# A four-layer graph network on one core: where a relu, the totals rows, some casts and the small weight loads stand, and how cell weights are loaded

## Chip, cores and metric

The kernel runs on one core of a Trainium2 chip. The metric is device time in microseconds of one execution; lower is better. The engines are named as the profile names them: PE multiplies matrices (PEld is its weight load), DVE is the vector engine, ACT the scalar engine, POOL is GpSimd, SP issues DMAs.

## What is computed

3327 nodes with 64 features go through four residual layers. Each layer normalizes its input, applies a relu, propagates over the same adjacency matrix and adds the result to `x`.

```python
def _ggc(x, adj, W, wih, whh, bih, bhh):
    m = adj @ (x @ W)
    gi = m @ wih.T + bih
    gh = x @ whh.T + bhh
    i_r, i_z, i_n = jnp.split(gi, 3, axis=-1)
    h_r, h_z, h_n = jnp.split(gh, 3, axis=-1)
    r = jax.nn.sigmoid(i_r + h_r)
    z = jax.nn.sigmoid(i_z + h_z)
    n = jnp.tanh(i_n + r * h_n)
    return (1.0 - z) * n + z * x
# layer 0: relu(_ggc(relu(_ggc(h, adj, cell 1)), adj, cell 2))
# layer 1: weights 0.5 ** (how many neighbours stand behind this one in the row,
#          the last 100 only), times (h @ weight), plus bias
# layer 2: three times  x = (adj * adj) @ x;  x = x @ W.T + b
# layer 3: twice  x = tanh(concat(adj @ x, x) @ W[k])
# each layer: h = max(layernorm(x), 0);  x = x + layer(h, adj)
```

So the adjacency is used eight times: two plain passes (the two GRU cells), one ranked pass (layer 1), three squared passes and two plain ones.

## The kernel before

The nodes are padded to 3328, 26 blocks of 128 rows. A tile is one block of source rows against half of the destination columns: group 0 holds chunks 0 and 1 (3 blocks each), group 1 holds chunks 2 and 3 (3 and 4 blocks). With its two halves of destinations a tile of group 0 is 768 KB, one of group 1 is 896 KB. There are 20 slots for tiles in SBUF, and most tiles are loaded several times. A joint loop runs two passes over the same tiles, so that a load serves both: `alone(0, 0)`, then `joint(1, 0)` (passes 0 and 1 on group 1), `joint(0, 1)` (passes 1 and 2 on group 0), `joint(1, 2)`, and so on to `alone(0, 7)`. Pass 2 is the ranked one.

The order of the instructions on each engine is that of the program's text as it is emitted: every engine runs its own list in that order. The text is interleaved by hand. The main loop `run` emits units (pass, chunk, tile) of matmuls. Everything else, such as what follows the last tile of a chunk, is a generator that `yield`s an amount of microseconds; each unit "spends" its own share of matmul time on the open generators (`STREAM_US * w / CWM`, 0.645 for a plain unit of three blocks, 0.806 for a ranked one), and a generator whose amount is used up emits its next piece. A larger number after `yield` thus means that the next piece stands later in the lists of its engines, whatever the clock says.

The pieces that the change touches:

- `more_constants` (line 190) sets up constants in the background. `load_cell` (148) loads the weights of a GRU cell with four DMAs: W and the three input gates twice into `folds` (lines 152), once for each half of the partitions, and the three hidden gates twice into `cells` (153). The bias columns `bcol` are loaded twice (199). `fold_cell` (155) multiplies W with the input gates on PE, with a factor 0.5, since both halves of the partitions hold the same weights. `bd` and `w3` (232, 234) are the weights of layers 1 to 3, six small DMAs.
- `make_mask` (405) turns a tile into a bf16 mask of nonzeros for the ranked pass, in two pieces on DVE (411, one for each half); the pieces wait in a queue and are emitted one or more for each unit. Row 127 of the mask is not a mask but the row counts `totals`, which POOL copies in by DMA (416), emitted with the first piece.
- `expand` (429) makes ranks out of masks: PE multiplies the mask with a triangle `tri` (a `mm`, line 255), and a relu takes the result from PSUM to an int16 tile `e`, on ACT (461) or DVE (459). It runs three units ahead of the matmuls that use `e` (546).
- `gru` (781) is the cell: the accumulators are copied out (741, 742), PE forms the gates (792), ACT the sigmoids and the tanh (797, 813), DVE the rest (802 to 819). After cell 0 the relu of the new state is written in two halves, one on ACT (822), one on DVE (823); then `after_0` brings it back to nodes with matmuls (707).
- `after_1` (870) follows cell 1: `gru`, transposes, residual, `layernorm_relu` (its power is on POOL, 761), and `in_three` (829), which splits the result in three bf16 terms for the ranked pass: two casts on ACT (841), two subtractions on DVE (843).

## Time and profile before

| | |
|---|---|
| time, median of 3 runs | 721.32 us (717.43 to 722.89) |
| span of the profiled run | 714.8 us |
| granted TensorE clock | 1.00 |
| HBM read | 199.68 MB, 281 GB/s over the span |

The page gives for each engine its busy time, then slices of the span, queues, the chain that ended last, and the costliest groups. Matmuls in float32 are two records each, and the ends of matmuls are modelled, so a busy PE may still be waiting a little; gaps in the timeline tell more. The matmuls with the adjacency (line 546) are the largest group by far. The rest of the large groups is the work that feeds the ranked and the squared passes:

```profile
L546 PE MATMUL sum<-adj,y 128*64 128x384 f32 (+3 forms) x3016 | 532.6, 503 | 13.2 <-DMA adj<-in_adjT 12.2
L546 PE MATMUL sum<-e,adj 128*64 128x384 bf16 (+1 forms) x624 | 72.6, 339 | 0.6 <-DVE e L459 0.6
L388 ACT ACTIVATE adj<-adj 128x768 f32<-128x768 f32 (+1 forms) x173 | 141.9, 891 | 50.3 <-PE sum L546 26.9
L411 DVE TENSOR_SCALAR adj<-adj 128x768 bf16<-128x768 f32 (+3 forms) x208 | 114.8, 603 | 33.5 <-PE temp L481 29.6
```

A row reads: line, engine, operation, what it writes and reads, the commonest shape, how many; busy us and mean ns of one; idle time of its engine just before, and who ended it.

### The profile page before, as it was taken

Reading aid. Unit: us, or ns where it says so; the run is one execution under the profiler, and the core shown is the slowest. Engines: PE = TensorE matmul, PEld = TensorE weight load, DVE = VectorE, ACT = ScalarE, POOL = GpSimd, SP = SyncE. Lnnn points to the kernel's source line nnn. Section 1 sums busy time; section 2 is a strip of 40 time slices with the busy share of each in tenths; the row PEclk is TensorE's granted clock in tenths of the full one; section 3 lists DMA queues with packets and bytes.
Section 4 is the critical chain, followed back from the end, with each engine's and each line's share of the span. In section 5 each row is a group of like instructions: output and inputs, shape, how many; then the busy total and the mean of one; then the engine's idle time right before and its main releaser. Section 6 shows DMA issues by size and latency. Waiting matters only on the chain.

```text
span 714.8 us, 12622 instructions
## 1 busy us (share of the span) xinstructions
PE 685.6 (96%) x5112; PEld 344.0 (48%) x5112; DVE 344.0 (48%) x696; ACT 264.1 (37%) x402; POOL 76.7 (11%) x113
## 2 busy tenths in 40 slices
PE   4999899999999898999999999999999999999997
PEld 1545444555546586545444444334444444334464
DVE  6756636634987988658524102321163566005101
ACT  0114000212037666888998223740065600000101
POOL 3500000001390602121100000000010000000000
PEclk9999999999999999999999999999999999999999
DMA  9999996299586367662999749962998399927991
GB/s 347 401 363 404 405 406 196 64 351 397 186 298 236 115 205 262 211 239 72 313 368 366 255 146 408 405 263 79 375 373 259 113 397 405 404 82 263 403 402 39
DMA packets 69109, 201.54 MB, mean 282 GB/s; under 512 B 7404, under 2 KB 8788, under 8 KB 69052
## 3 DMA queue, kind: packets, MB, share of 16 engines
q1 hardware_dynamic: 66156, 199.70, 75.4%
q8 instruction: 40, 0.66, 0.4%
q10 hardware_dynamic: 720, 0.85, 0.3%
q0 software_dynamic: 2176, 0.20, 0.2%
q14 instruction: 17, 0.14, 0.1%
HBM read 199.68 MB, written 0.85 MB: 281 GB/s over the span
## 4 chain that ended last, share of the span: by engine, by line
PE 55%; DVE 2%; DMA 2%; ACT 0%; issue 0%; POOL 0%; ACTq 0%; DVEq 0%; SPq 0%; POOLq 0%
PE sum L546 51%; PE temp L255 3%; DMA adj<-totals 1%; PE temp L707 1%; DMA adj<-in_adjT 1%; DVE adj L411 1%; DVE both L742 0%; ACT both L741 0%; DVE e L459 0%; POOL st L761 0%; PE sum L255 0%; DVE xs L940 0%; DVE y L765 0%; DVE y L758 0%; DVE t L753 0%
## 5 line engine op out<-in xcount | busy, mean ns | idle before, releaser
L546 PE MATMUL sum<-adj,y 128*64 128x384 f32 (+3 forms) x3016 | 532.6, 503 | 13.2 <-DMA adj<-in_adjT 12.2
L546 PEld LDWEIGHTS sum<-adj,y 128*64 128x64 f32 x3016 | 221.5, 137 | 267.8 <-issue 223.9
L388 ACT ACTIVATE adj<-adj 128x768 f32<-128x768 f32 (+1 forms) x173 | 141.9, 891 | 50.3 <-PE sum L546 26.9
L411 DVE TENSOR_SCALAR adj<-adj 128x768 bf16<-128x768 f32 (+3 forms) x208 | 114.8, 603 | 33.5 <-PE temp L481 29.6
L461 ACT ACTIVATE e<-temp,bitsb 128x384 int16<-128x384 f32 (+1 forms) x114 | 65.3, 606 | 23.5 <-PE temp L255 14.6
L546 PE MATMUL sum<-e,adj 128*64 128x384 bf16 (+1 forms) x624 | 72.6, 339 | 0.6 <-DVE e L459 0.6
L742 DVE COPY both<-sum 64x384 f32<-64x384 f32 (+3 forms) x17 | 9.7, 569 | 118.7 <-ACT both L741 117.5
L741 ACT COPY both<-sum 64x384 f32<-64x384 f32 (+3 forms) x17 | 8.1, 477 | 155.2 <-PE sum L546 155.1
L390 DVE TENSOR_TENSOR adj<-adj 128x768 f32<-128x768 f32 (+1 forms) x35 | 33.6, 1006 | 51.1 <-DMA adj<-in_adjT 30.9
L255 PE MATMUL temp<-adj,tri 128*64 128x384 bf16 (+1 forms) x334 | 51.9, 342 | 5.5 <-DVE e L459 2.3
L761 POOL TENSOR_TENSOR st<-st,mhalf 128x6 f32<-128x6 f32 (+1 forms) x16 | 24.0, 1500 | 295.5 <-DVE st L760 295.5
L546 PEld LDWEIGHTS <-adj 128*64 128x64 bf16 x624 | 40.4, 110 | 18.5 <-issue 6.4
L416 POOL DMA_DIRECT2D adj<-totals x52 | 31.9, 615 | 133.5 <-DVE adj L819 75.0
L459 DVE TENSOR_SCALAR e<-temp 128x384 int16<-128x384 f32 (+1 forms) x53 | 31.8, 606 | 21.2 <-ACT e L461 8.6
L255 PEld LDWEIGHTS <-tri 128*64 128x64 bf16 x416 | 28.6, 109 | 25.8 <-issue 12.8
L736 DVE STREAM_TRANSPOSE both<-y 32x96 f32<-32x96 f32 (+1 forms) x128 | 35.6, 278 | 2.9
L688 DVE COPY t<-sum 128x384 f32<-128x384 f32 x8 | 4.4, 555 | 61.3 <-PE sum L546 61.3
L481 PE MATMUL temp<-adj,behind 128*64 128x384 bf16 x208 | 28.8, 339 | 0.6 <-DVE adj L411 0.4
L686 ACT COPY t<-sum 128x384 f32<-128x384 f32 (+1 forms) x8 | 4.2, 528 | 53.7 <-PE sum L546 53.7
L481 PEld LDWEIGHTS <-behind 128*64 128x64 bf16 x208 | 13.6, 110 | 21.1 <-issue 19.5
L903 DVE TENSOR_TENSOR y<-temp,brow 128x384 f32<-128x384 f32 (+1 forms) x8 | 4.7, 591 | 29.6 <-PE temp L255 29.6
L515 ACT ACTIVATE lastw<-adj,bitsb 128x768 int16<-128x768 f32 (+1 forms) x2 | 2.0, 984 | 44.1 <-DVE adj L513 44.1
(113 smaller groups left out, 330.1 us busy)
## 6 DMA issues: line engine op xcount, KB each, us to landing
adj<-in_adjT SPq DMA_DIRECT2D x130, 768.0 KB, 7.8
adj<-in_adjT SPq DMA_DIRECT2D x104, 896.0 KB, 12.4
xs<-in_x SPq DMA_DIRECT2D x1, 640.0 KB
adj<-totals POOLq DMA_DIRECT2D x26, 3.0 KB, 4.9
adj<-totals POOLq DMA_DIRECT2D x26, 3.5 KB, 3.0
out<-xs ACTq DMA_DIRECT2D x2, 192.0 KB, 4.0
folds<-in_weights SPq DMA_DIRECT2D x4, 64.0 KB, 12.1
out<-xs ACTq DMA_DIRECT2D x1, 256.0 KB
```

What stands on the lines that cost most here:

```text
L255: nc.tensor.matmul(out[hs], lhsT[:, hs], rhs, start=start, stop=stop)
L388: nc.scalar.activation(sq, v, AF.Square)
L390: nc.vector.tensor_tensor(sq, v, v, ALU.mult)
L411: nc.vector.tensor_scalar(t.mask.view[:rows, half], t.view()[:rows, half], 0.0, None, op0=ALU.not_equal)
L416: nc.gpsimd.dma_start(out=t.mask.view[P - 1:P], in_=totals[t.g][t.q:t.q + D + 1:D, :])
L459: nc.vector.tensor_scalar(wide[:, s], ps[:, :w], BITS, 0.0, op0=ALU.add, op1=ALU.max)
L461: nc.scalar.activation(wide[:, s], ps[:, :w], AF.Relu, bias=bitsb)
L481: nc.tensor.matmul(counts[c][1][s * D:(s + 1) * D, :w], behind[:, NQ - 1 - t.q:NQ - 1 - t.q + D], t.mask.view[:, s, t.cols(c)], start=firs ...
L546: nc.tensor.matmul(acc[h][1][h * D:(h + 1) * D, :w], yq[h], rhs[h], start=first and n == 0, stop=last and n == len(terms) - 1)
L736: nc.vector.transpose(to[at:at + 32, :, q], h[q * 32:(q + 1) * 32, :, s, f * 32:(f + 1) * 32])
L742: nc.vector.tensor_copy(both[c][upper(1), 1], acc[1][1][upper(1), :width(c)])
L761: nc.gpsimd.tensor_tensor(st[:, 3, :n], st[:, 2, :n], mhalf[:, :n], ALU.pow)
```

## The change

It rearranges what is small. The cell weights and the bias come once, into a tile `stage` that is zero in its lower half, and PE and DVE copy them to both halves of the partitions (`unfold_cell`); `fold_cell` works from `stage`. `bd` and `w3` are loaded after the second cell has been folded, and later. The DVE half of the cell's relu stands before the yield, and that yield is a little longer. The row of totals is asked for when the mask is planned, not with its first piece. Some relus of `expand` go from ACT to DVE: in group 1, the second half of tiles whose source is chunk 2. The casts of `in_three` stand later, and `after_1` has one pace of 1.25 for both groups.

```diff
-    folds = const.tile([P, 2, 4, D], F32, name="folds")
+    stage = const.tile([P, 7 * D + NBIAS], F32, name="stage")
...
     def load_cell(cell):
-        w, hh = ((W1, HH1), (W2, HH2))[cell]
-        for h in range(2):
-            nc.sync.dma_start(out=folds[upper(h), cell], in_=weights[:, w:w + 4])
-            nc.sync.dma_start(out=cells[upper(1 - h), cell, h, 0:3], in_=weights[:, hh:hh + 3])
+        nc.sync.dma_start(out=stage[upper(0), :7 * D].rearrange("p (w f) -> p w f", f=D),
+                          in_=weights[:, (W1, W2)[cell]:(W1, W2)[cell] + 7])
+        if cell == 0:
+            nc.sync.dma_start(out=stage[upper(0), 7 * D:], in_=bias_cols)
+
+    def unfold_cell(cell):
+        n = 3 * D + (NBIAS if cell == 0 else 0)
+        i, ps = take()
+        for h in range(2):
+            nc.tensor.matmul(ps[upper(h), :n], ident[:, :D], stage[:, 4 * D:4 * D + n], start=True, stop=True)
+        v = ps[:, :3 * D].rearrange("p (g f) -> p g f", f=D)
+        for h in range(2):
+            nc.vector.tensor_copy(cells[upper(1 - h), cell, h, 0:3], v[upper(1 - h)])
+        if cell == 0:
+            nc.vector.tensor_copy(bcol, ps[:, 3 * D:n])
+        give(i)
 
     def fold_cell(cell):
         i, ps = take()
-        for h in range(2):
-            nc.tensor.matmul(ps[upper(h), :P], folds[:, cell, 0], ident, start=True, stop=True)
+        for n in range(2):
+            for h in range(2):
+                nc.tensor.matmul(ps[upper(h), upper(n)], stage[:, :D], ident[:, :D], start=True, stop=True)
         tr = work.tile([P, P], F32, name="t2")
-        nc.scalar.activation(tr, ps[:, :P], AF.Copy, scale=0.5)
+        nc.scalar.copy(tr, ps[:, :P])
...
-        mm(ps[:, :3 * D], tr, folds[:, cell, 1:4].rearrange("p g f -> p (g f)"))
+        mm(ps[:, :3 * D], tr, stage[:, D:4 * D])
...
     def more_constants():
+        nc.gpsimd.memset(stage, 0.0)
...
         load_cell(0)
-        for h in range(2):
-            nc.sync.dma_start(out=bcol[upper(h)], in_=bias_cols)
         yield 20.0
+        unfold_cell(0)
+        yield 1.0
...
         yield 50.0
         load_cell(1)
-        yield 10.0
+        yield 20.0
+        unfold_cell(1)
+        yield from fold_cell(1)
+        yield 40.0
         for h in range(2):
             nc.sync.dma_start(out=bd[upper(h), :, upper(h)], in_=weights[:, WL1:WL3])
             for i in range(2):
                 nc.sync.dma_start(out=w3[upper(h), :, i], in_=weights[:, WL3 + (h + i) % 2:NW:2])
-        yield 10.0
-        yield from fold_cell(1)
-        yield 20.0
+        yield 5.0
...
         def piece(half):
             nc.vector.tensor_scalar(t.mask.view[:rows, half], t.view()[:rows, half], 0.0, None, op0=ALU.not_equal)
-            if half == 0 and kind == RANKED:
-                for ch in GROUPS[t.g]:
-                    finish(("count", ch))
-                nc.gpsimd.dma_start(out=t.mask.view[P - 1:P], in_=totals[t.g][t.q:t.q + D + 1:D, :])
             if half == 1:
                 t.used()
+        if kind == RANKED:
+            for ch in GROUPS[t.g]:
+                finish(("count", ch))
+            nc.gpsimd.dma_start(out=t.mask.view[P - 1:P], in_=totals[t.g][t.q:t.q + D + 1:D, :])
         pieces.extend([(t, 0, piece), (t, 1, piece)])
...
-            if s and (own if t.g == 0 and (own or busy) else c == GROUPS[t.g][1] or t.g == 1 and not own):
+            alone = own and chunk_of(t.q % NB) == GROUPS[1][1]
+            if s and (own if t.g == 0 and (own or busy) else c == GROUPS[t.g][1] or t.g == 1 and not alone):
...
         nc.vector.tensor_tensor(d, d, r, ALU.add)
-        yield 2.2 * pace
+        if cell == 0:
+            nc.vector.tensor_scalar(both[c][upper(0), 1], d[upper(0)], 0.0, None, op0=ALU.max)
+        yield 2.4 * pace
         if cell == 0:
             nc.scalar.activation(both[c][upper(1), 0], d[upper(1)], AF.Relu)
-            nc.vector.tensor_scalar(both[c][upper(0), 1], d[upper(0)], 0.0, None, op0=ALU.max)
-            yield 1.0 * pace
+            yield 1.0
...
-    def in_three(h, c):
+    def in_three(h, c, pace=1.0):
...
-            yield 0.8
+            yield 1.2 * pace
             nc.scalar.copy(terms[i], h)
...
     def after_1(c, acc):
-        pace = 1.0 if c in GROUPS[0] else 1.2
+        pace = 1.25
```

## The prediction

> **What bounds the kernel now.** I read the page first. PE is busy in 96% of the span, so a change can win only what PE loses in waits or in added matmuls.
>
> ```profile
> span 714.8 us, 12622 instructions
> PE 685.6 (96%) x5112; PEld 344.0 (48%) x5112; DVE 344.0 (48%) x696; ACT 264.1 (37%) x402; POOL 76.7 (11%) x113
> DMA  9999996299586367662999749962998399927991
> ```
>
> PE spends 29.2 us idle (714.8 - 685.6), some 13 of them at the start and the end. In the DMA row the queue is full for the first six slices (107 us) and has holes later. The windows (columns: PE, PEld, DVE, ACT, POOL busy with counts, clock, DMA share, GB/s) say where PE's other idle time lies.
>
> ```profile
> 40.00:60.00 20.00, 18.84 (x140) 8.63 (x138) 11.51 (x28) 2.04 (x5) 0.00 (x0) 1.00 1.02 393
> 60.00:80.00 20.00, 17.72 (x152) 11.37 (x150) 16.25 (x32) 7.88 (x14) 0.00 (x0) 1.00 1.03 405
> 220.00:240.00 20.00, 17.83 (x214) 12.23 (x211) 17.91 (x37) 12.73 (x25) 3.51 (x5) 1.00 0.53 194
> 240.00:260.00 20.00, 18.40 (x213) 14.69 (x214) 18.91 (x39) 16.34 (x32) 8.25 (x13) 1.00 0.58 201
> 360.00:380.00 20.00, 19.72 (x132) 8.65 (x130) 8.99 (x12) 20.00 (x26) 0.00 (x0) 1.00 0.99 370
> ```
>
> From 380 us to the end PE stands full, and the change touches nothing there. So three places count: the arrival-bound start, the first GRU cell at 60 to 80, and the ranked stage from 220 to 340, where DVE is nearly full. The timeline gives single waits, in brackets the idle time and its releaser:
>
> ```profile
> 43.09 0.20 PEld L546 LDWEIGHTS sum<-adj,y 128*64 128x64 f32 x4 [1.23 <-DMA adj<-in_adjT]
> 72.23 0.56 DVE L819 TENSOR_TENSOR adj<-adj 128x384 f32<-128x384 f32 x1
> 75.10 0.56 DVE L819 TENSOR_TENSOR adj<-adj 128x384 f32<-128x384 f32 x1
> 76.65 0.34 DVE L823 TENSOR_SCALAR both<-adj 64x384 f32<-64x384 f32 x1
> 77.05 0.80 PE L707 MATMUL sum<-ident,both 128*64 128x64 f32 x20 [2.13 <-DVE both L823]
> 124.08 0.62 SPq L232 DMA_DIRECT2D bd<-in_weights  x1
> 129.82 0.87 PE L546 MATMUL sum<-adj,y 128*64 128x384 f32 x4 [1.28 <-DMA adj<-in_adjT]
> ...
> 281.48 1.32 POOL L761 TENSOR_TENSOR st<-st,mhalf 128x6 f32<-128x6 f32 x1 [7.03 <-DVE st L760]
> 282.76 1.20 POOL L416 DMA_DIRECT2D adj<-totals  x2
> 283.91 1.15 DVE L411 TENSOR_SCALAR adj<-adj 127x896 bf16<-127x896 f32 x2
> 284.99 0.52 PE L255 MATMUL temp<-adj,tri 128*64 128x384 bf16 x4 [1.10 <-DMA adj<-totals]
> 329.01 5.43 DVE L411 TENSOR_SCALAR adj<-adj 127x896 bf16<-127x896 f32 x10
> ```
>
> At 77.05 PE waits for a relu whose input has been there since 72.8.
>
> [...] small weight loads issued from 26.5 us land 6 to 14 us later, behind adjacency tiles. [...] here the rows of totals land in 1.6 to 6.0 us (median 4.0). [...] at 237 to 241 us ACT stands 3.69 us in front of L841 while relus wait behind it. That makes the place of an instruction in the text matter.
>
> **Part by part.**
>
> *Loads of cell 0.* PE takes tiles as they land, 1.95 us apart (waits at 16.01 and 17.96). Between the tiles at 35.95 and 43.09 lie three such steps (5.85 us) and six small loads; 7.14 - 5.85 = 1.29 us, 0.21 each. Two stay, one of them 64 x 1792 B = 115 KB, an estimated 0.28 us at 405 GB/s: 0.5 us together. PE waits for tiles until 50.95, so this shift reaches it: -0.8 us. Bounds: 0 to -1.0.
>
> *Unfolding and folding.* Eight extra matmul records per two cells, 205 or 192 columns; four of 128x192 take 0.49 us at 50.35 with overlap, so 0.35 us a cell. The first lies in the arrival-bound stretch; the second, near 147 us, is on a full PE: +0.35. Folding has the same columns in twice as many records: +0.1. DVE's copies of 64x192 lie between 64x128 (0.288) and 64x384 (0.55), 0.36 each, 1.6 us with the bias; DVE is 11.5 of 20 busy at 40 to 60 and 6.7 at 140 to 160, so 0. The memset of stage, 0.8 us by the row of bd (128x512, 0.82), is on POOL, for which PE waits nowhere: 0. The new wait of `unfold_cell(0)` for its load holds nothing: it stands where L215 waited only 0.35 us for the bias, and it sits behind fewer loads.
>
> *Relu of the cell (L823) ahead of the yield.* It then ends at 73.2 and 76.0 for the two chunks; PE asked at 74.9. The other half, ACT L822, was done at 73.4. The wait of 2.13 us goes: -2.1. L411 is queued behind it on DVE, 0.34 us later, and PE needs those masks two tiles later. After 80 us PE is full (20.00 of 20) while the loads run ahead of it, so the gain is carried on. Bounds: -0.8 (DVE's own idle time there, 0.82) to -2.3.
>
> *bd and w3 loads 52 us later.* Six small loads at 124 to 127 share the engines with the tile issued at about 123.5, for which PE waits 1.28 us at 129.82. At 0.21 each, six cost 1.26: -1.2. They go to about 188 us, where DMA share is 0.60 and PE waits for no tile until 212: 0. First use of bd is at 266.9. The loads of cell 1, four to one, lie where PE is full: 0.
>
> *Row of totals ahead of the mask pieces.* In the steady state POOL already stands at L416 waiting for PE to free the slot (20.1 us on L255 in nine waits), so an earlier place gives nothing. At 282.76 it stood behind the pow L761; earlier it would be landed in time, but PE also needs the first half of the mask, DVE L411, done at about 284.55: only 0.4 of the 1.1 us goes: -0.4. At 316.67 the slot is the limit: 0.
>
> *Six relus (own sources of chunk 2) from ACT to DVE.* 0.58 us each, 3.4 us. At 307 to 318 DVE has 6.5 us of idle time (3.14 and 3.36), and the first ones are free. From 318 a tile takes 1.89 us and DVE 1.84 of it; three or four relus there push the ten L411 at 329, behind which PE starts at 334.85. ACT gains 3.4 us, but PE is full at 360 to 380 beside a full ACT. Bounds: -1 (squares sooner) to +2; I take +0.7.
>
> *Paces of after_1 and in_three.* Sum of the yields from the last tile of a chunk to the last term: 5.8 + 0.8 + 4.8 + 3.2 = 14.6 before for group 0, 18.5 now. PE needs the terms after 4 units of 0.645 and 24 of 0.806, 21.9 in the same count, so it fits by 3.4. But DVE works without a pause from 221.6 to 252: its total sets the time of this stretch, and spreading the same work over it takes none away. Bounds: -2.5 to +3.9; I take 0. The later copy L841 lets ACT do a relu first, behind the same DVE.
>
> Sum: -0.8 + 0.35 + 0.1 - 2.1 - 1.2 - 0.4 + 0.7 = -3.35; 721.3 - 3.35 = 718.0.
>
> **Rivals.** *The ranked stage gains too: 713.* The waits of PE at 220 to 260 are 3.8 us (2.17 + 1.60). With chains spread, 2.5 of them go, all 2.2 us of waits on totals instead of 0.4, and the relus cost nothing: 3.35 + 0.7 + 1.8 + 2.5 = 8.35. For it: the ACT wait of 3.69. Against: the full DVE.
>
> *Arrivals take the early gains back: 721.* DMA is saturated until about 95 us; if tiles land when they did, the 0.8 and 2.1 are lost: 718.0 + 2.9 = 720.9. Against: PE falls behind the loads after 80 us.
>
> *Slower: 731.* The terms come 3.9 us late and all of it shows, DVE's 3.4 us of relus too, and two pows wait on POOL behind a totals row that waits for PE (20.1 / 9 = 2.2 to 2.9 us each, 5.8 together): 13.1 against 3.65 of early gains (3.35 without the 0.4 and 0.7): +9.45. For it: POOL is in order and rows now stand ahead of pows. Against: a row's slot is freed by matmuls that stand earlier in the text.
>
> **How the numbers follow.** Forecast 0.38 (718.0), ranked stage 0.33 (713), arrivals 0.17 (721), slower 0.12 (731). Single runs of before spread 2.7 us to either side (717.43 to 722.89). Low end: 713 - 2.7 = 710; high end: 721 plus the same and part of the slower case, 726. What lies outside is most of the 0.12 and a tail of the 0.33. 1% is 7.2 us, so faster begins at 714.1: two thirds or more of the 0.33 and a twelfth of the rest, 0.30. Slower begins at 728.5: 0.12. Between: 0.58.
>
> **What would show it.** Right: no wait of PE L707 on L823 near 75; tiles at 43 less than 0.5 us late; no wait near 128 on adj; PE at 380 some 4 us earlier. Wrong: that wait replaced by one on L411 or adj; PE idle at 220 to 260 below 2 us (the rival at 713) or above 6; POOL's pow behind L416 with DVE L765 waiting; the L411 row at 329 longer and PE idle with it.

## The result, and the profile after

The changed kernel takes 725.43 us (median of 13 runs, 723.97 to 728.62), the kernel before 720.84 us in the same comparison (13 runs, 717.43 to 724.93): the ratio is 1.0062, with an interval of 1.0044 to 1.0081. The change costs 4.6 us where the forecast was a gain of 3.35. The time lies in the range of 710 to 726, near its upper end; the direction was wrong.

Line numbers move with the change: L546 is now L562, L255 is L270, L411 is L426, L416 is L434, L459 and L461 are L475 and L477, L804 is L820, L770 is L786, L761 is L777, L823 is L837. First the page of the changed kernel, the lines that answer to those of before:

```profile
span 724.8 us, 12652 instructions
PE 690.2 (95%) x5128; PEld 357.1 (49%) x5128; DVE 349.5 (48%) x707; ACT 261.4 (36%) x396; POOL 82.6 (11%) x114
DMA  9999995198685358472699929980997399926991
```

PE is busy 4.6 us longer and the span is 10.0 us longer, so idle time and slower matmuls both grew. The 10.0 us between the two traces are more than the 4.6 us between the times; a second trace of the kernel before (below), with a span of 719.3 us, shows that the first one was a lucky execution. Four of the windows that the prediction shows, now in the changed kernel (PE, PEld, DVE, ACT, POOL busy with counts, clock, DMA share, GB/s):

```profile
40.00:60.00 20.00, 19.34 (x150) 9.02 (x148) 12.21 (x31) 1.91 (x5) 0.00 (x0) 1.00 1.03 399
60.00:80.00 20.00, 19.12 (x158) 11.27 (x154) 17.36 (x34) 7.90 (x14) 0.00 (x0) 1.00 1.03 405
220.00:240.00 20.00, 16.38 (x200) 12.13 (x198) 14.43 (x27) 12.94 (x27) 1.94 (x3) 1.00 0.46 150
240.00:260.00 20.00, 16.35 (x191) 12.78 (x187) 19.54 (x43) 14.20 (x28) 9.97 (x14) 1.00 0.42 139
```

The early stretches have less idle PE than before (0.66 and 0.88 us instead of 1.16 and 2.28). The stretch 220 to 260 has more: 3.62 + 3.65 = 7.27 us instead of 3.77. And DVE, full before in 220 to 240 with 17.91 us, has only 14.43, while PE does less: the total of DVE does not set this stretch.

Where the lead is lost is read best from the start of the same matmul in both traces. The matmuls that use the ranks (`sum<-e,adj`) are counted from 0; times are us:

| place | before | after | lead lost up to here | lost in this step |
|---|---|---|---|---|
| no. 0 | 205.65 | 203.41 | -2.24 | -2.24 |
| no. 24 | 219.93 | 221.71 | +1.78 | +4.02 |
| no. 192 | 253.48 | 257.86 | +4.38 | +2.60 |
| no. 360 | 282.07 | 286.42 | +4.35 | -0.03 |
| no. 384 | 288.35 | 295.45 | +7.10 | +2.75 |
| no. 480 | 320.57 | 330.32 | +9.75 | +2.65 |
| no. 600 | 341.66 | 351.68 | +10.02 | +0.27 |

So the early gains are there, 2.24 us of them, and two steps take more than that back: one at 205 to 222 us, one at 222 to 258. The two jumps at 282 and 308 to 330 are the waits for the rows of totals, whose length differs between executions of one kernel.

**The first step, 205 to 222.** The queue of SP and the waits of PE in the changed kernel (start, duration, engine, line, operation, in brackets the idle time and its releaser):

```profile
196.81 0.62 SPq L249 DMA_DIRECT2D bd<-in_weights  x1
197.49 1.26 SPq L251 DMA_DIRECT2D w<-in_weights  x2
198.79 0.60 SPq L249 DMA_DIRECT2D bd<-in_weights  x1
199.44 1.27 SPq L251 DMA_DIRECT2D w<-in_weights  x2
200.82 2.14 SPq L368 DMA_DIRECT2D adj<-in_adjT  x2
203.01 0.60 SPq L253 DMA_DIRECT2D brow<-in_bias_rows  x1
...
210.65 0.87 PE L562 MATMUL sum<-adj,y 128*64 128x384 f32 x4 [1.90 <-DMA adj<-in_adjT]
212.86 2.62 PE L562 MATMUL sum<-adj,y 128*64 128x384 f32 x8 [1.34 <-DMA adj<-in_adjT]
```

Before there is one wait in this place, of 0.75 us at 212.40. Beside the small loads the bulk loads slow down, as the last two columns of the windows show. The kernel before, then the changed one:

```profile
201.00:203.00 2.00, 2.00 (x14) 0.84 (x12) 2.00 (x5) 0.62 (x1) 2.00 (x5) 1.00 0.83 282
```

```profile
201.00:203.00 2.00, 2.00 (x18) 1.08 (x16) 2.00 (x5) 1.81 (x4) 1.65 (x2) 1.00 0.71 114
```

114 GB/s instead of 282, for 2 us: the six loads of `bd` and `w3` are 1,024 packets of 256 B with a mean of 22.8 ns (the trace of the DMA engines at 199.9 to 202.6 us), 1.46 us of the time of each of 16 engines. In these 2.7 us the median packet of 256 B took 18 ns and one of 3,072 B 121 ns, so a byte took 1.8 times as long in the small ones.

The packets are not all of it. SP issues one load after the other, the six small ones keep it from 196.81 to 200.71, and the tile behind them is issued at 200.82, 4.60 us after the tile ahead of them. Before, the same two tiles are issued 3.15 us apart (198.46 and 201.61). How the loss splits between the packets and the later issue was not tested; both come from the place of the small loads.

**The second step, 222 to 258.** PE's longest waits there in the changed kernel:

```profile
230.68 0.52 PE L270 MATMUL temp<-adj,tri 128*64 128x384 bf16 x4 [2.07 <-DVE adj L820]
237.03 0.35 PE L270 MATMUL temp<-adj,tri 128*64 128x384 bf16 x2 [1.23 <-DVE xs L786]
243.20 0.35 PE L270 MATMUL temp<-adj,tri 128*64 128x384 bf16 x2 [1.53 <-DVE xs L786]
```

L820 and L786 are steps of the GRU chain and of the residual, and each of them reads a sum out of PSUM, after which its bank is given back. The matmul behind it (L270) reads a mask and `tri` and nothing that these lines write, so what it waits for is a free bank. In the kernel before the waits on these lines are 0.22 (L804, at 226.94) and 0.65 us (L770, at 235.50).

**Half clock.** The page shows the granted clock in tenths, 9 everywhere. In finer windows the changed kernel has three stretches of 3.4 us at half clock while the program runs, behind its waits for tiles (1.90 and 1.34 us at 210 to 213) and behind the two waits for rows of totals shown below, but none behind the wait of 2.07 us at 230.68. The first trace of before has none:

```profile
213.10:216.50 3.40, 3.40 (x14) 1.35 (x12) 1.72 (x4) 1.07 (x3) 1.81 (x4) 0.50 0.72 276
291.60:295.00 3.40, 3.40 (x15) 1.25 (x13) 2.16 (x4) 2.55 (x4) 0.54 (x1) 0.50 0.01 1
325.80:329.20 3.40, 3.40 (x16) 1.47 (x14) 1.80 (x4) 1.02 (x2) 0.54 (x1) 0.51 0.42 117
```

```profile
290.82 0.52 PE L270 MATMUL temp<-adj,tri 128*64 128x384 bf16 x4 [2.59 <-DMA adj<-totals]
324.73 0.52 PE L270 MATMUL temp<-adj,tri 128*64 128x384 bf16 x4 [2.07 <-DMA adj<-totals]
```

The column before the DMA share is the clock, 0.50. PE is "full" here with half the work: by an estimate, half of the 3.40 us, such a stretch costs 1.7 us. Of the step of 4.02 us at 205 to 222, 1.90 + 1.34 - 0.75 = 2.5 us are waits; the rest goes with the slow clock.

### The profile page after: what moved, and what is told of

It is laid out like the page before. It is cut to its first block, busy times and chain, and to the rows that moved or that the text cites. A ratio compares the mean times of both kernels' runs of the same rounds, so it can differ in the third digit from the quotient of the medians.

```text
span 724.8 us, 12652 instructions
## 1 busy us (share of the span) xinstructions
PE 690.2 (95%) x5128; PEld 357.1 (49%) x5128; DVE 349.5 (48%) x707; ACT 261.4 (36%) x396; POOL 82.6 (11%) x114
## 4 chain that ended last, share of the span: by engine, by line
PE 52%; ACT 4%; DVE 1%; DMA 1%; issue 1%; ACTq 0%; DVEq 0%
PE sum L562 48%; ACT adj L403 4%; PE temp L270 3%; DMA adj<-totals 1%; DVE adj L426 1%; PE temp L723 1%; DVE both L758 0%; ACT both L757 0%; ACT t L702 0%; PE sum L270 0%; DVE xs L957 0%; ACT e L477 0%; ACTq L959 0%; ACTq L403 0%; ACT t L954 0%
## 5 line engine op out<-in xcount | busy, mean ns | idle before, releaser
L562 PE MATMUL sum<-adj,y 128*64 128x384 f32 (+3 forms) x3016 | 537.3, 505 | 13.0 <-DVE y L781 8.6
L562 PEld LDWEIGHTS sum<-adj,y 128*64 128x64 f32 x3016 | 230.6, 138 | 263.3 <-issue 220.0
L426 DVE TENSOR_SCALAR adj<-adj 128x768 bf16<-128x768 f32 (+3 forms) x208 | 116.3, 609 | 31.9 <-PE temp L497 28.0
L562 PE MATMUL sum<-e,adj 128*64 128x384 bf16 (+1 forms) x624 | 73.1, 340 | 0.6 <-DVE e L475 0.6
L477 ACT ACTIVATE e<-temp,bitsb 128x384 int16<-128x384 f32 (+1 forms) x106 | 61.1, 601 | 34.7 <-PE temp L270 17.7
L270 PE MATMUL temp<-adj,tri 128*64 128x384 bf16 (+1 forms) x334 | 51.8, 351 | 12.3 <-DMA adj<-totals 4.7
L777 POOL TENSOR_TENSOR st<-st,mhalf 128x6 f32<-128x6 f32 (+1 forms) x16 | 24.3, 1519 | 292.7 <-DVE st L776 292.7
L434 POOL DMA_DIRECT2D adj<-totals x52 | 37.7, 726 | 139.9 <-DMA adj<-in_adjT 75.7
L562 PEld LDWEIGHTS <-adj 128*64 128x64 bf16 x624 | 41.2, 110 | 18.7 <-issue 6.8
L475 DVE TENSOR_SCALAR e<-temp 128x384 int16<-128x384 f32 (+1 forms) x61 | 36.3, 601 | 24.7 <-PE temp L270 13.4
L270 PEld LDWEIGHTS <-tri 128*64 128x64 bf16 x416 | 29.1, 112 | 32.7 <-issue 17.9
L497 PE MATMUL temp<-adj,behind 128*64 128x384 bf16 x208 | 31.3, 340 | 2.4 <-DVE adj L426 2.3
L497 PEld LDWEIGHTS <-behind 128*64 128x64 bf16 x208 | 18.2, 110 | 18.6 <-issue 16.2
L531 ACT ACTIVATE lastw<-adj,bitsb 128x768 int16<-128x768 f32 (+1 forms) x2 | 2.0, 984 | 42.6 <-DVE adj L529 42.6
```

Of the source, the lines that this page charges most:

```text
L270: nc.tensor.matmul(out[hs], lhsT[:, hs], rhs, start=start, stop=stop)
L426: nc.vector.tensor_scalar(t.mask.view[:rows, half], t.view()[:rows, half], 0.0, None, op0=ALU.not_equal)
L434: nc.gpsimd.dma_start(out=t.mask.view[P - 1:P], in_=totals[t.g][t.q:t.q + D + 1:D, :])
L475: nc.vector.tensor_scalar(wide[:, s], ps[:, :w], BITS, 0.0, op0=ALU.add, op1=ALU.max)
L477: nc.scalar.activation(wide[:, s], ps[:, :w], AF.Relu, bias=bitsb)
L497: nc.tensor.matmul(counts[c][1][s * D:(s + 1) * D, :w], behind[:, NQ - 1 - t.q:NQ - 1 - t.q + D], t.mask.view[:, s, t.cols(c)], start=firs ...
```

## The experiments

**The five parts alone, each on the kernel before.** The weights (staging, unfolding, folding, and all the loads as the change places them):

```diff
-        w, hh = ((W1, HH1), (W2, HH2))[cell]
-        for h in range(2):
-            nc.sync.dma_start(out=folds[upper(h), cell], in_=weights[:, w:w + 4])
-            nc.sync.dma_start(out=cells[upper(1 - h), cell, h, 0:3], in_=weights[:, hh:hh + 3])
+        nc.sync.dma_start(out=stage[upper(0), :7 * D].rearrange("p (w f) -> p w f", f=D),
+                          in_=weights[:, (W1, W2)[cell]:(W1, W2)[cell] + 7])
...
         load_cell(1)
-        yield 10.0
+        yield 20.0
+        unfold_cell(1)
+        yield from fold_cell(1)
+        yield 40.0
         for h in range(2):
             nc.sync.dma_start(out=bd[upper(h), :, upper(h)], in_=weights[:, WL1:WL3])
```

> The kernel before with the weights alone changed (stage, unfold, fold, later bd, w3 and brow). Theory A (the six loads of bd and w3 and brow now stand in a stretch where each adjacency tile is loaded just in time): PE is 1.2 to 1.5 us ahead at 200 us, then waits 3 us more than before for adj at 205 to 215; about 723 us. Theory B (the tiles are late there because slots are held longer by the slower chain of after_1): no such wait, about 719.5 us.

Measured: 723.63 us, ratio 1.0054 (1.0027 to 1.0080). This group alone is slower, and its trace has a wait of 2.47 us for a tile at 215.29.

The relu of the cell's upper half ahead of the yield:

```diff
-        yield 2.2 * pace
+        if cell == 0:
+            nc.vector.tensor_scalar(both[c][upper(0), 1], d[upper(0)], 0.0, None, op0=ALU.max)
+        yield 2.4 * pace
```

> The kernel before with the DVE half of the cell's relu ahead of the yield alone. The wait of PE L707 on L823 (2.13 us) is gone; theory A: a wait for masks (DVE L411) of about 0.8 us takes part of its place, 0.9 to 1.4 us are won at 90 us and kept: about 719.7 us. Rival: the same is lost again in the ranked stage, 720.8 us.

Measured: 718.06 us, ratio 0.9970 (0.9952 to 0.9988). Faster, by 2 us and so by more than theory A; the clock accounts for the difference (see "Why the prediction was wrong"). The yield of 2.4 holds for the second cell too; the stretch from no. 24 to no. 192 takes 33.55 us with it and 33.54 without, so it costs nothing there.

The row of totals ahead of the mask pieces:

```diff
-            if half == 0 and kind == RANKED:
...
+        if kind == RANKED:
+            for ch in GROUPS[t.g]:
+                finish(("count", ch))
+            nc.gpsimd.dma_start(out=t.mask.view[P - 1:P], in_=totals[t.g][t.q:t.q + D + 1:D, :])
```

> The kernel before with the rows of totals asked for earlier alone. Theory A (the rows are late in the changed kernel because they now stand elsewhere on POOL): the two waits of PE on rows grow from 1.1 and 1.1 to 2.6 and 2.1 us, 2.5 us or more slower, 723.5 us. Theory C (they are late because a shift in time laid them on another transfer): rows and waits as before, 720.8 us within 1.

Measured: 721.89 us, ratio 1.0022 (1.0000 to 1.0043). Between the two theories, and on the edge of the noise. PE's waits on rows in its trace, 3.08 and 1.88 us, are about those of the second trace of the kernel before (3.03 and 1.73), so they do not tell for theory A; the runs on the rows below return to it.

The paces of `after_1` (1.25 for all) and of `in_three` (1.2 instead of 0.8):

```diff
-            yield 0.8
+            yield 1.2 * pace
...
-        pace = 1.0 if c in GROUPS[0] else 1.2
+        pace = 1.25
```

> The kernel before with the slower paces of after_1 and in_three alone. Theory A (a slower chain holds banks of PSUM longer, and PE waits for a bank): waits of PE L255 on DVE L802 and L770 at 225 to 245, PE 2.5 us later at 255, about 723.4 us. Rival (the stretch is set by the total work of DVE): no change at 255, 720.8 us.

Measured: 724.49 us, ratio 1.0061 (1.0035 to 1.0088). Slower, and PE's wait on the GRU line is in its trace too, with 2.06 us.

The split of the sixteen-bit relus between ACT and DVE:

```diff
-            if s and (own if t.g == 0 and (own or busy) else c == GROUPS[t.g][1] or t.g == 1 and not own):
+            alone = own and chunk_of(t.q % NB) == GROUPS[1][1]
+            if s and (own if t.g == 0 and (own or busy) else c == GROUPS[t.g][1] or t.g == 1 and not alone):
```

> The kernel before with only the rule that hands six of the sixteen-bit relus of RANKED expand units from ScalarE to VectorE. Theory of the three losses (late small loads, slower paces, half-clock stretches after waits): this edit has no part in any of them, so 720.8 us like the kernel before, ratio 0.998 to 1.003. Rival, that my +0.7 us for these six relus was right or too small because VectorE has no pause between 221 and 252 us: 721.5 to 723, ratio 1.001 to 1.003. Another rival, that the five parts do not add up and the split carries what the parts run so far leave over: over 723.

Measured: 720.41 us, ratio 0.9996 (0.9976 to 1.0016). Nothing. The five add up to +0.54 - 0.30 + 0.22 + 0.61 - 0.04 = +1.03%; the whole has +0.62%, and with five intervals of about 0.2 either way the two agree. A part of the difference is that the rows and the paces do not add up (see the table of stretches below).

**The kernel before once more**, for a second trace:

> The kernel before, unchanged, for a second trace. Theory D (the long waits on the rows of totals at about 285 and 317 us and the clock at a half for 3.4 us after such a wait come in some executions and not in others, the changed kernel's among them): this trace shows waits of another length than 1.1 us there, up to 3 us, and where one is over some 1.9 us a stretch at half clock after it; span 714 to 723 us. Rival (both belong to the change): the waits are 1.1 us again and the clock is 1.000.

Measured: 721.19 us, span 719.3 us. PE's wait for the row of totals, and the window after it:

```profile
287.44 0.85 PE L255 MATMUL temp<-adj,tri 128*64 128x384 bf16 x4 [3.03 <-DMA adj<-totals]
```

```profile
287.50:290.90 3.40, 3.40 (x18) 1.49 (x18) 0.93 (x2) 2.33 (x4) 0.17 (x1) 0.51 0.02 5
```

The same kernel waits 3.03 us and then runs at half clock where its first trace waited 1.10 us and did not. So steps like those of 2.75 and 2.65 us at 282 to 330 in the table can come without a change of the code; what the change costs has to be read from the times and from the other two steps.

**One loss undone at a time, in the changed kernel.** First `bd`, `w3` and `brow` back to the early place:

```diff
         load_cell(1)
-        yield 20.0
+        yield 10.0
+        for h in range(2):
+            nc.sync.dma_start(out=bd[upper(h), :, upper(h)], in_=weights[:, WL1:WL3])
...
+        yield 10.0
         unfold_cell(1)
         yield from fold_cell(1)
-        yield 40.0
-        for h in range(2):
-            nc.sync.dma_start(out=bd[upper(h), :, upper(h)], in_=weights[:, WL1:WL3])
...
-        yield 5.0
+        yield 20.0
```

> The changed kernel with the loads of bd, w3 and brow back near their first place (10 us after load_cell(1), brow 20 us after the fold). Theory A (these loads cost 3 to 4 us at 205 to 215 us): the two waits on adj there shrink to one of about 1 us, PE gains 3 us or more by 222 us: about 722.3 us. Theory B (held slots): no change, 725.4 us.

Measured: 722.04 us, ratio 1.0001 (0.9978 to 1.0024). In its trace the waits of 1.90 and 1.34 us are gone, and one is left:

```profile
211.45 1.51 PE L562 MATMUL sum<-adj,y 128*64 128x384 f32 x8 [0.93 <-DMA adj<-in_adjT]
```

Then the old paces with the late loads kept (`pace = 1.0 if c in GROUPS[0] else 1.2`, yields of 0.8):

> The changed kernel with the paces of after_1 and in_three as before. Theory A: the waits on L820 and L786 for banks of PSUM at 230 to 245 go, 2.5 us won there: about 722.5 us. Theory B (slots held by the slower chain also make the tiles late at 210): 4 us or more won: 721 us or below. Rival (the total of DVE): no change, 725.4 us.

Measured: 723.52 us, ratio 1.0030 (1.0007 to 1.0052). Its trace still has a wait of 2.47 us on an adjacency tile at 213.41, so slots held longer by slower chains are not what delays the tiles. The lead lost between no. 24 and no. 192 is 0.6 us instead of 2.6, and the rows of totals account for these 0.6 (below).

**The loads by themselves.** The staged weights with the small loads early, on the kernel before:

> The kernel before with only the new staging of the cells' weights (stage, unfold, fold), and with the loads of bd, w3 and brow left where the kernel before has them, ahead of the fold. The run with the weights group as a whole took 723.63 us, 0.5% more than the kernel before. Theory (the loss of that group is the late issue of the small loads at 197 to 203 us into a stretch where each adjacency tile comes just in time): with the loads early the loss of about 3 us goes, and the start's small gain (-0.5 to -0.8 us) stays: 719.5 to 721 us, ratio 0.998 to 1.001. Rival (the unfold copies on VectorE and the wait of TensorE on the staged weights at 77 us cost it): still 722.5 to 724 us, ratio 1.003 to 1.005.

Measured: 720.77 us, ratio 0.9996 (0.9976 to 1.0016). Without the late loads the weights cost nothing, but the hoped gain of 0.5 us does not show either. And only the late loads, with the old `folds` and `cells`:

```diff
         load_cell(1)
-        yield 10.0
+        yield 20.0
+        yield from fold_cell(1)
+        yield 40.0
         for h in range(2):
             nc.sync.dma_start(out=bd[upper(h), :, upper(h)], in_=weights[:, WL1:WL3])
...
-        yield 10.0
-        yield from fold_cell(1)
-        yield 20.0
+        yield 5.0
         nc.sync.dma_start(
             out=brow[:, 0:3],
```

> The kernel before with one edit: bd, w3 and brow are loaded after the fold of the second cell and a yield of 40, as in the changed kernel, everything else as before. Theory (the lateness of these seven loads is the whole loss of the weights group): 723 to 725 us, ratio 1.003 to 1.006. Rival (the loss needs the staged weights beside it): 720 to 721.5 us, ratio 0.999 to 1.002.

Measured: 724.36 us, ratio 1.0046 (1.0024 to 1.0068). The two waits are back:

```profile
213.29 0.87 PE L546 MATMUL sum<-adj,y 128*64 128x384 f32 x4 [1.01 <-DMA adj<-in_adjT]
216.12 2.83 PE L546 MATMUL sum<-adj,y 128*64 128x384 f32 x8 [1.97 <-DMA adj<-in_adjT]
```

The place of seven loads is the whole loss of the weights group, as far as the intervals tell (1.0046 and 1.0054).

**Which pace.** The yields of `in_three` alone, then `pace = 1.25` alone:

> The kernel before with one edit: the two yields ahead of the copies in in_three go from 0.8 to 1.2. Both paces together gave 724.49 us, ratio 1.006. Theory (the loss is the chain of after_1 for the first group, which holds sums in their banks for longer): about none of it, 720 to 722 us, ratio 0.999 to 1.003. Rival (in_three holds the next ready tile back): 723 us or more, ratio 1.003 or above.

> The kernel before with one edit: the pace of after_1 is 1.25 for all chunks instead of 1.0 for the first group and 1.2 for the second. Theory: most of the loss of the two paces, 723 to 725 us, ratio 1.003 to 1.006, with TensorE's waits on VectorE at 230 to 245 us longer than in the kernel before. Rival (in_three carries it): 720 to 722 us, ratio 0.999 to 1.003.

Measured: 722.08 us, ratio 1.0008 (0.9991 to 1.0026), for `in_three`; 724.32 us, ratio 1.0039 (1.0019 to 1.0059), for `after_1`. PE's wait on the same instruction (`adj` of the GRU, L804) in the kernel with the old pace of `after_1`, then in the one with 1.25:

```profile
229.61 0.92 PE L255 MATMUL sum<-ident,adj 128*64 128x64 f32 x24 [0.22 <-DVE adj L804]
```

```profile
234.11 0.52 PE L255 MATMUL temp<-adj,tri 128*64 128x384 bf16 x4 [2.06 <-DVE adj L804]
245.84 0.35 PE L255 MATMUL temp<-adj,tri 128*64 128x384 bf16 x2 [0.99 <-DVE xs L770]
```

The pace of the chain in `after_1` carries the loss, between steps that hold a PSUM bank. From no. 24 to no. 192 PE waits 7.29 us in all with 1.25 and 3.73 before; 1.84 of the added 3.56 us are on L804.

**Both undone.** The changed kernel with early small loads and old paces:

> The changed kernel with both suspected causes undone: the small loads bd, w3 and brow early as before, and the paces of after_1 and in_three as before. What stays of the change: staged weights, relu of the upper half, rows of totals, split of the sixteen-bit relus. Theory (late loads and slower paces are the whole of the loss): 717.5 to 719.5 us, ratio 0.995 to 0.999, near the 718.45 us of the same kernel without the rows and the split. Rival (a third cause is left, or the two undone parts overlap): 721 us or more, ratio 1.000 or above.

Measured: 720.45 us, ratio 0.9995 (0.9980 to 1.0010). The theory's 0.995 to 0.999 is missed at its edge: two losses are not all, since the staged weights with the relu alone are at 0.9973 (the last run below). The times also show less for the paces beside early loads (1.0001 to 0.9995) than beside late ones or alone, with intervals of 0.0015 to 0.0023 either way. The traces show a smaller part of that: 36.16 to 34.18 us from no. 24 to no. 192, 2.0 us, where the pace alone adds 2.8.

**The rows of totals, a third loss.** The relu with the rows, on the kernel before, and the kernel of the last run without the rows:

> The kernel before with the moved relu and the rows of totals issued earlier, nothing else. Theory (the rows cost 0.2%): about 720 us, ratio 0.998 to 1.000, against 0.997 for the relu alone; the trace shows one TensorE wait of about 1.2 us near 238 us on VectorE's sixteen-bit relu where the relu alone shows 0.6. Rival (the rows cost nothing): 718 to 718.8 us, ratio 0.996 to 0.9975.

> The changed kernel with three parts undone: the small loads early, the old paces, and the rows of totals issued with the first half of a mask as before. What stays: staged weights, the moved relu, the split of the sixteen-bit relus. Theory (the rows are a third loss of 0.2%): 718.0 to 719.0 us, ratio 0.996 to 0.998, as the kernel with staged weights and relu alone. Rival (the difference of 0.2% between those kernels was noise): 720 to 720.8 us, ratio 0.999 to 1.000.

Measured: 720.63 us, ratio 1.0003 (0.9982 to 1.0023), for relu and rows, where the relu alone has 0.9970; 719.33 us, ratio 0.9977 (0.9957 to 0.9997), without the rows, where the kernel with them has 0.9995. With the rows alone (1.0022) that is three pairs, +0.33, +0.18 and +0.22%, of one sign; none of them alone is beyond doubt. The traces show one wait that comes with the rows. Relu alone, DVE, POOL and PE:

```profile
235.88 0.18 DVE L752 TENSOR_SCALAR st<-st 128x6 f32<-128x6 f32 x1
...
235.20 0.83 POOL L503 MEMSET adj<- 128x896 f32 x1
235.99 0.60 POOL L416 DMA_DIRECT2D adj<-totals  x1
...
237.71 0.35 PE L255 MATMUL sum<-adj,tri 128*64 128x384 bf16 x2 [0.58 <-DVE e L459]
```

Relu and rows:

```profile
234.80 0.81 DVE L752 TENSOR_SCALAR st<-st 128x6 f32<-128x6 f32 x1
...
234.12 0.60 POOL L419 DMA_DIRECT2D adj<-totals  x1
234.71 0.86 POOL L503 MEMSET adj<- 128x896 f32 x1
...
237.26 0.35 PE L255 MATMUL sum<-adj,tri 128*64 128x384 bf16 x2 [1.21 <-DVE e L459]
```

With the row issued first, the memset of POOL starts 0.09 us ahead of a DVE instruction of 0.18 us instead of 0.68 us ahead of it; the instruction then takes 0.81 us and ends just after the memset (235.61 and 235.57), and PE waits 0.63 us longer. Among the twenty traces of this study exactly the seven of kernels with the moved rows have one such stretched DVE instruction at 230 to 240 us. In the changed kernel it is a mask piece of 0.62 us that takes 1.58, ahead of L786, for which PE waits at 237.03:

```profile
234.93 1.58 DVE L426 TENSOR_SCALAR adj<-adj 127x896 bf16<-127x896 f32 x1
...
234.63 0.54 POOL L434 DMA_DIRECT2D adj<-totals  x1 [1.79 <-PE sum L270]
235.17 0.86 POOL L519 MEMSET adj<- 128x896 f32 x1
```

Here the piece is recorded 0.24 us ahead of the memset, not behind it; why the two instructions are stretched is not shown. Nor does it cost anything beside the slower pace: from no. 24 to no. 192 the kernels with both take 36.15 and 36.16 us, those with the pace alone 36.27 and 36.31. In this stretch the rows are a third loss only where the pace is the old one; there they cost 0.63 us (0.09%). The waits for rows from no. 360 to no. 480 may hold more: that stretch takes 40.9 to 44.6 us in the six traces with moved rows and 38.4 to 42.6 in the twelve without (those with filling, below, left out). That this is the rows' doing is not shown.

**The price of the slow clock.** Twelve useless matmuls (bf16, 512 columns) ahead of each of the two ranked units in question in the changed kernel, so that PE's wait for the row of totals is filled:

```diff
+        if len(ranked_units) - 1 in (64, 80):
+            i, ps = take()
+            for _ in range(6):
+                mm(ps, tri, totals[0][:, :CWM])
+            give(i)
```

> The changed kernel with 12 useless bf16 matmuls of 512 columns (1.3 us of PE) ahead of each of the two matmuls that wait for rows of totals at about 290 and 325 us. Theory D (a wait of PE of 2 us or more is followed by 3.4 us at half clock, and that costs as much again): the idle waits shrink by 1.3 us each, less of the half clock follows, the mean clock rises by 0.002 to 0.004 and the time falls by 2 to 3 us although work is added: about 723 us. Rival (the half clock has no part in the time): the same time, 725.4 us, or up to 2.6 us more where the rows are there already.

Measured: 724.36 us, ratio 1.0015 (0.9988 to 1.0042). The wait shrinks, and no half clock follows:

```profile
291.88 0.52 PE L270 MATMUL temp<-adj,tri 128*64 128x384 bf16 x4 [1.76 <-DMA adj<-totals]
```

```profile
291.60:295.00 3.40, 2.12 (x18) 1.05 (x20) 1.98 (x4) 2.68 (x4) 0.54 (x1) 1.00 0.01 1
```

The mean clock of its runs is 0.9969 against 0.9932 for the changed kernel. By medians the gain on the changed kernel is 1.1 us, by the ratios 3.4 us (0.47%), with intervals that just part (1.0042 and 1.0044); a gain in spite of added matmuls, of uncertain size and smaller than the theory's by the medians. The same filling on top of the relu:

> The kernel before with the relu of the upper half moved, and with twelve matmuls that compute nothing used ahead of the RANKED expand units 64 and 80, where TensorE otherwise waits 2 to 3 us for the row of totals. Theory (a wait of about 2 to 3 us makes the granted clock fall to half for 3.4 us, which costs about 1.7 us more each time): the clock stays nearer to full in those places, mean 0.998 or more, and the time is 716.5 to 718 us, ratio 0.994 to 0.997. Rival (the twelve matmuls only fill the wait and the clock costs nothing there, or they come late and add their own 2.5 us): 718 to 720.5 us, no less than the relu alone at 718.06.

Measured: 718.75 us, ratio 0.9970 (0.9957 to 0.9983), the same as the relu alone. The clock rose from 0.9984 to 0.9992 only. So the rival is right here: with the relu moved there was little left to win, and the added matmuls cost as much.

**A version that beats both.** Staged weights, early small loads and the moved relu:

> The kernel before with the staged weights, the small loads where they were, and the relu of the upper half moved ahead of the yield; the paces, the rows of totals and the split of the sixteen-bit relus as before. Theory: the two parts that help without the two that cost. The relu alone gave 718.06 us (0.997); with the weights' early gain of up to 0.8 us: 717 to 718.5 us, ratio 0.995 to 0.998, faster than both kernels. Rival (the stage's gains early in the run are taken back by the arrival of adjacency tiles before 200 us): the same 720 to 721 us as the kernel before.

Measured: 718.45 us, ratio 0.9973 (0.9957 to 0.9989). Faster than both kernels, and not to be told from the relu alone (0.9970). As far as the times can tell, one line moved ahead of a yield is all that the change has to give.

**The same stretches in all twenty traces.** Each stretch runs from the start of one matmul to that of another. Adjacency means the matmuls `sum<-adj,y`, ranked those of the table further up, both counted from 0. Times in us, in brackets the number of traces:

| stretch | part | with the part | without |
|---|---|---|---|
| start to adjacency no. 180 | staged weights | 53.28 to 54.05 (9) | 53.91 to 54.92 (10), 57.23 (1, half clock) |
| adjacency 180 to 240 | moved relu | 24.61 to 24.80 (10) | 25.71 to 25.89 (4), 26.84 to 27.51 (6, half clock) |
| adjacency 420 to 480 | late small loads | 16.85 to 17.19 (5) | 17.06 to 18.02 (15) |
| adjacency 480 to 700 | second unfolding, new fold | 54.24 to 54.27 (9) | 53.89 to 53.91 (11) |
| ranked 0 to 24 | late small loads | 16.48 to 19.36 (5) | 13.79 to 15.71 (15) |
| ranked 24 to 192 | `after_1` pace 1.25 | 36.15 to 36.31 (5) | 33.48 to 33.56 (11), 34.14 to 34.19 (4, moved rows) |
| ranked 480 to 600 | six relus to DVE | 21.30 to 21.36 (7) | 21.09 to 21.10 (13) |

So each loss stands in its own stretch: 3.25 us in the mean for the late loads (17.95 and 14.70), 2.8 us for the pace. The gain of the relu is 1.1 us, and 1.6 us more where its wait cost the clock.

## Why the prediction was wrong

*Loads of cell 0 and the unfolding: right in size, too small for the times.* The nine traces with staged weights reach the adjacency matmul no. 180 at 53.62 us in the median, the eleven others at 54.49: 0.9 us earlier (predicted -0.8). The second unfolding and the fold take back 0.36 us (predicted 0.35 + 0.05). What is left is too small for the runs (0.9996) to show.

*Relu ahead of the yield: right in the sum, wrong in its parts.* PE's wait of 2.13 us on L823 goes, and the one that "Wrong" named comes in its place, on the mask pieces that now queue behind it:

```profile
76.67 0.32 PE L497 MATMUL temp<-adj,behind 128*64 128x384 bf16 x1 [0.52 <-DVE adj L426]
77.20 0.32 PE L497 MATMUL temp<-adj,behind 128*64 128x384 bf16 x1 [0.21 <-DVE adj L426]
```

From matmul no. 180 to no. 240 the relu alone gains 1.09 us, the changed kernel 0.92; I had taken 2.1. The times give more, 0.30% or 2.2 us, and the clock accounts for the rest: of ten traces with the relu in its old place six have a half-clock stretch at 77 to 80 us behind this wait, of the ten with it moved none. At 1.6 us in six of ten cases that is 1.0 us, 2.1 with the wait itself. That the sum came out as predicted is luck: the clock had no part in the prediction.

*`bd` and `w3` out of the early place: right in kind, too large.* The wait of 1.28 us at 129.82 is gone; the lead grows from 1.44 to 2.61 us between matmuls no. 420 and 480, which looks like the predicted 1.2. But the first trace of before is the slowest of all there (18.02 us; the second takes 17.43). The mean is 17.03 us with the loads moved and 17.55 with them early: 0.5 us.

*`bd` and `w3` into the late place: the step that failed.* I wrote "They go to about 188 us, where DMA share is 0.60 and PE waits for no tile until 212: 0". They were issued from 196.81 on, the last at 200.10, and `brow`, which I had not placed, at 203.01. And "PE waits for no tile until 212" was read as slack. It was the opposite: no wait, but no lead either, for the next one at 212 shows that tiles come just in time, with DMA at 0.83 to 0.95 at 200 to 209 us. I had priced the same six loads at 1.26 us in their old place, and 0 in the new one; the packets alone took 1.46 us, PE's waits and the slow clock behind them the rest. Measured: 0.5% or 3.5 us (the pairs +0.54, +0.46, and undone -0.58, -0.61 and -0.35%).

*Paces: the other step that failed.* "DVE works without a pause from 221.6 to 252: its total sets the time of this stretch": I took 0 within bounds of -2.5 to +3.9. The trace of before has two pauses of DVE there (0.71 and 0.22 us), and from no. 24 to no. 192 DVE idles 5.02 us in the changed kernel against 2.73 before, while PE waits more (7.27 us against 3.77). What binds, by the wait on L804 (0.22 us with the old pace of `after_1`, 2.06 with 1.25), is how long a chain step holds its PSUM bank, so a longer pause between steps goes into PE's wait: 2.60 us in the trace, 0.06 to 0.61% in the runs. The rise in `in_three`, which I worked out with care to fit by 3.4 us, does indeed fit (1.0008). Of the signs of being wrong that the prediction lists, one is this: PE idle above 6 us at 220 to 260, where it was 7.27.

*Rows of totals: wrong sign, small.* -0.4 us predicted, about +0.2% (1.5 us) measured, of which 0.63 us is placed. I looked for what waits for the row, and not for what the earlier row moves on POOL. PE's wait on it at unit 64, whose length I took from one trace (1.10 us), is anything from 1.1 to 3.5 us in the traces of this study.

*Six relus to DVE: right to leave small.* +0.7 within -1 to +2; the times give 0.0 with an interval of 1.4 us either way, the traces +0.26 us from no. 480 to no. 600.

The slower rival, 731 us, named the terms coming late as its cause with +3.9; half of what happened was there, but through the PSUM banks and not through the terms. The other half, small loads beside just-in-time tiles, was in none of the cases. In the sum: -2.24 + 4.02 + 2.60 = +4.4 us in the traces up to no. 192, and +4.6 us in the times. That the two agree so closely is chance, since single traces of one kernel differ by more: against the second trace of before it is 257.86 - 253.98 = +3.9.

## What to carry to other kernels

Small loads had a price in the queue here (3.25 us in the mean for the late ones), so find for their new place not only whether anyone waits there now but whether the tiles have a lead; a stretch with no wait and a busy DMA just before a wait was the costly place here. A longer pause between the steps of a chain that held PSUM banks cost 2.8 us here, and the one between the casts of `in_three` cost nothing that the times show (1.0008). So ask of a chain whether it holds something that the bounding engine wants back: look at which steps read PSUM, not at how busy their engine is. And take a second trace of the kernel before: one execution can be some us from the median, and a single wait (1.10 and 3.03 us here) can be anywhere.

## What the runs showed of the hardware

In the changed kernel the granted clock falls to half (0.50) three times, for 3.41 us each, after waits of PE that are shorter than that: one of 2.07 us was enough (at 324.73), where another of 2.07 us was not (at 230.68).

In every trace the starts of the half-clock stretches lie whole multiples of 3.413 us apart (78.51 and 34.13 us in the changed kernel, 23 and 10 of them). Along that grid, from 30 to 690 us of all twenty traces, 26 windows at full clock are followed by half clock; PE was idle in them for 1.98 to 3.05 us. The 3,812 others at full clock, with at most 2.00 us idle, are not. So in these traces the idle time within one window tells the two apart, at about 2.0 us, and where the grid falls against a wait differs from one trace to the next. The wait of 2.13 us at 77 lay in one window in the six traces that lost the clock (2.11 to 2.13 us of it), and the grid cut it in the four others (at most 1.91 us idle in one window). The kernel with relu and rows waited 2.93 us for its row, cut in half, and kept full clock; the second trace of before waited 3.03 us within one window and lost it. So a wait of 2 us cost itself here and, where it lay in one window, an estimated 1.7 us more, half of the 3.41. Over the 48 runs of the kernel before in one comparison the time falls by 0.8 us for each 0.001 of mean clock (correlation -0.78); the waits that lower the clock are part of that.

On DVE, ACT, POOL and SP the first traces of both kernels show the instructions in the order in which the program emits them (696, 405, 113 and 257 of them before, 707, 399, 114 and 250 after). The 1,508 float32 matmuls of L546 are 3,016 records in the trace of before.

Beside a memset of 0.86 us on GpSimd that starts 0.09 us ahead of it, a VectorE instruction of 0.18 us took 0.81. Another of 0.62 us took 1.58 beside such a memset, though it is recorded as starting 0.24 us ahead of it. A row of totals of 3 to 3.5 KB took from 1.6 to 6.0 us from issue to landing in the kernel before. In the changed kernel one took 12.0, and 7.29 us of that are POOL's own instruction, with a median of 0.54 us:

```profile
202.28 7.29 POOL L434 DMA_DIRECT2D adj<-totals  x1 [0.35 <-PE temp L270]
```

Five of the seven traces with moved rows have one such POOL instruction of 6.6 to 7.3 us, three of them with the small loads early, and none of the thirteen others has. In each of the five it stands beside fifteen mask pieces of DVE in a row (7.1 us). In the kernel before POOL issues its rows beside the same fifteen pieces without such a delay, so why it is held stays open.
